# A graph layer on one core: transposes of node windows by a DRAM round trip and VectorE, and six units' rows fetched one by one from SyncE's queue

## The chip, the cores and the metric

The kernel runs on one core of a Trainium2 chip. The metric is the device time of one execution in microseconds (us). Engines are named as in the profile: PE (TensorE, matmuls), PEld (its weight loads), DVE (VectorE), ACT (ScalarE), POOL (GpSimd), SP (SyncE, which here issues DMAs; SPq is its DMA queue).

## The reference

One layer of a graph network with N = 6250 nodes, D = 256 features and E = 206250 edges that are sorted by their destination `dst`:

```python
h = jnp.maximum(_layernorm(x, axis=-1), 0.0)
polarity = jnp.clip(edge_attr[:, 0:1], 0.0, 1.0)
raw = edge_attr[:, 1:]                                  # [E, 64]
e = jax.nn.relu(raw @ W_e1.T + b_e1) @ W_e2.T + b_e2
gated = e * (polarity + 0.01)
edge_emb = gated @ W_le.T + b_le
msg = jax.nn.relu(h[src] + edge_emb)                    # [E, 256]
aggr = jax.ops.segment_sum(msg, dst, num_segments=N)
g = (h + aggr) @ W_g1.T + b_g1
mu, var = mean and variance of g over its row
hn = (g - mu) * jax.lax.rsqrt(var + LN_EPS) * ln_g + ln_b
out = x + jax.nn.relu(hn) @ W_g2.T + b_g2
```

All data are float32. W_e2 and W_le have only a scaling by edge between them, so the kernel multiplies with one product of the two (`wc_s`).

## The kernel before

**Edges.** Edges are laid in tiles of 128. A *unit* is 2 tiles, a *block* 2 units, a *group* L = 6 blocks, that is GU = 12 units; there are 806 units in 67 full groups and a rest. The main loop runs over units, `u` from LEAD = 22 to 805. For each unit stand, in the order of the engines' work:

- POOL gathers the rows `h[src]` of a unit out of DRAM (`hb_d`), with two indirect DMAs (L722), into one of 25 buffers: 17 named `hg`, 8 named `hx`. They are issued about two groups ahead, whenever a buffer is free, and a buffer is free again when the sums (L806) have read it.
- PE makes relu's argument of the first layer (L338), three pairs of units at once at the end of each group; ACT (L353) and DVE (L350) move the results out of PSUM to `e`.
- PE multiplies `e` with `wc_s` (L372: four matmuls of a unit, eight records in the profile) into a PSUM bank that ACT has filled with the bias (L402, "seed").
- DVE multiplies with the polarity and adds the gathered rows, in place (L755, two instructions a unit); ACT applies relu (L766, one instruction).

At the last unit of a group (`u % 12 == 11`) PE adds the messages up by destination (L806): 64x32 selection matrices, which DVE has built (L737), times messages. ACT (L824) and DVE (L825) move the sums into `ms`. SP then writes them to DRAM (`sum_d`), in four DMAs of 32 rows whose addresses come out of registers (`rows_out`: L905 loads the registers, L910 writes); the program makes each of the four wait for the one before. SP also clears later parts of `sum_d` (L899).

The first KEPT = 24 units are different: their products stay in tiles `msg`, because PE makes them while `h` is not yet in DRAM. Units 8 to 23 of them get their rows later, by ordinary POOL gathers set into the stream "beside" every EVERY = 36th unit, from unit 42 to 582; DVE and ACT finish them then (`whole_kept`, L778).

**Nodes.** Nodes are treated in *windows* of 128 rows. When all groups that touch a window are added up, `far_work(w)` lays out its steps over the next units. There are 47 such windows. 42 use the ordinary pools; 5 use tiles of kept units that are free by then (L173 and L214 read `msg` there), and 3 of these 5 are "filling": their last two steps are kept for the end of the program. The steps are: load `x`, and the relu of its norm (L941); load the sums (L943, SP); add both (L946, DVE, two instructions); then

- `turned`: PE transposes the [128 x 256] tile `stb` by two matmuls with an identity (L173), and ACT copies the result from PSUM to SBUF (L177, `hT`);
- `one`: the first product with `wg_s` (L188, two matmuls, four records), DVE adds the bias (L196) and takes the row statistics;
- `rooted`, `normed`: the norm (L207, L208, result `hs`);
- `two`: PE transposes `hs` (L214, two matmuls), and ACT applies scale, bias and relu on the way out of PSUM (L218, two instructions, `nT`);
- `three`: the second product (L227, four records), DVE adds `x` (L232), SP writes the output (L235).

**What sets the order.** A recording layer fixes the order of instructions on each engine as the Python code calls them; every engine then runs its list in order and waits by semaphores. Steps of windows are called after a unit's own work: `soon(n, f)` calls `f` n units later, `at(u, f)` puts it in a list of which one entry is called for each unit, and none in the units where `u % 12` is 11 or 0 (`due`). The stages above are chained by `run` with gaps of (2, 1, 1, 2, 3) units, from 12 units after the window is complete, so that a window's stages all follow one group's sums.

## Time and profile before

| | us |
|---|---|
| three runs | 3829.58, 3826.62, 3807.94 (median 3826.62) |
| the profiled execution | 3820.48 |
| its span in the profile | 3818.7 |
| PE busy | 3030.0 (79%) |
| DVE busy | 1315.3 (34%) |
| ACT busy | 1295.4 (34%) |
| POOL busy | 1563.9 (41%) |

The mean granted clock of PE was 0.789. The span is the time from the first to the last profiled instruction; the 1.8 us between it and the execution's time lie around it. A row of the timeline reads: start, duration, engine, line, operation, output<-input, shape, count, and in brackets the idle time just before it and what ended that. Engine rows of one kind that follow each other are merged, so "x4" with 5.50 us holds four instructions and what lay between them. In a row of the groups, the numbers behind the bar are the busy time of all, the mean of one in ns, and the idle time ahead of them with its releasers. "remote" and "issue" are waits for which the profile shows no engine.

### The profile page before, as it was taken

The page shows a single profiled execution, that of the slowest core. Times are in us where ns is not written, and L with a number is a line of the kernel's source. Part 1 is how long each engine was busy: PE and PEld are TensorE (multiplying, and loading weights), DVE is VectorE, ACT ScalarE, POOL GpSimd, SP SyncE. Part 2 cuts the span into 40 slices and gives each one's busy share as a digit, 9 for nine tenths or more (in the row PEclk, how much of TensorE's full clock was granted, in tenths as well). Part 3 has the DMA queues.
Part 4 walks back from the last instruction along what each step waited for, and adds up shares of the span by engine and source line. Part 5 has one row for each costly group of instructions (what it writes and reads, how often), then busy time and mean ns, then how long its engine had stood idle before and what let it go on. Part 6 is the DMA issues. An engine that isn't in the chain of part 4 may idle for free.

```text
span 3818.7 us, 51854 instructions
## 1 busy us (share of the span) xinstructions
PE 3030.0 (79%) x19998; PEld 1840.7 (48%) x19998; DVE 1315.3 (34%) x2970; ACT 1295.4 (34%) x2408; POOL 1563.9 (41%) x1674
## 2 busy tenths in 40 slices
PE   8477787788787787788787788787787888787788
PEld 5344454454455454454455455455454455455446
DVE  5343233242233232233233233233233343233234
ACT  5243233243233232333233233233242343233234
POOL 7434434424434434434433434433434434433431
PEclk9787787787787787787787787787787787787788
DMA  7322222223223222223322222322222222222321
GB/s 252 103 74 81 83 85 84 84 74 92 87 79 89 85 81 79 83 79 90 90 82 77 86 80 83 95 82 73 89 82 88 83 82 81 86 82 79 88 76 44
DMA packets 143718, 331.53 MB, mean 87 GB/s; under 512 B 36000, under 2 KB 71417, under 8 KB 142713
## 3 DMA queue, kind: packets, MB, share of 16 engines
q0 software_dynamic: 77376, 211.39, 19.2%
q1 hardware_dynamic: 64788, 113.47, 9.7%
q8 instruction: 159, 2.61, 0.3%
q10 hardware_dynamic: 1300, 3.29, 0.3%
q14 instruction: 95, 0.77, 0.1%
HBM read 306.25 MB, written 34.08 MB: 89 GB/s over the span
## 4 chain that ended last, share of the span: by engine, by line
PE 66%; another core or an unknown queue 16%; issue 14%; DVE 2%; ACT 2%; DMA 1%; POOL 0%; DVEq 0%; ACTq 0%; POOLq 0%
PE pz L372 41%; PE pz L806 13%; PE pz L338 9%; PE pz L188 1%; PE pz L227 1%; PE pz L173 1%; DVE hg L755 1%; ACT hg L766 1%; ACT pz L402 0%; PE pz L214 0%; ACT ms L824 0%; DVE sel L737 0%; DVE msg L778 0%; DMA hg<-hb_d,src_s 0%
## 5 line engine op out<-in xcount | busy, mean ns | idle before, releaser
L372 PE MATMUL pz<-wc_s,e 128*128 128x256 f32 x6448 | 1857.5, 439 | 407.0 <-issue 331.4
L372 PEld LDWEIGHTS pz<-wc_s,e 128*128 128x128 f32 x6448 | 1387.7, 220 | 861.4 <-issue 589.3
L722 POOL DMA_INDIRECT hg<-hb_d,src_s x1096 | 1038.3, 947 | 1394.3 <-PE pz L806 856.6
L722 POOL DMA_INDIRECT hx<-hb_d,src_s x500 | 473.6, 947 | 789.5 <-PE pz L806 461.3
L825 DVE TENSOR_TENSOR ms<-ms,pz 128x256 f32<-128x256 f32 x68 | 28.7, 421 | 1842.9 <-remote 715.0
L806 PE MATMUL pz<-hg,sel 64*32 64x256 f32 x4312 | 520.6, 406 | 174.7 <-issue 147.1
L824 ACT ACTIVATE ms<-pz 128x256 f32<-128x256 f32 x68 | 26.0, 383 | 1791.0 <-remote 1700.4
L755 DVE SCALAR_TENSOR_TENSOR hg<-pz,pol_s,hg 128x256 f32<-128x256 f32 x1078 | 467.4, 479 | 352.9 <-PE pz L372 90.2
L766 ACT ACTIVATE hg<-hg 128x512 f32<-128x512 f32 x538 | 337.7, 628 | 401.3 <-DVE hg L755 351.8
L402 ACT ACTIVATE pz<-bc_s 128x512 f32<-128x512 f32 x782 | 453.2, 586 | 0.0
L806 PEld LDWEIGHTS pz<-hg,sel 64*32 64x32 f32 x4312 | 164.8, 108 | 487.9 <-issue 457.8
L338 PE MATMUL pz<-raw,we_s 64*32 64x512 f32 x6448 | 377.5, 596 | 7.8 <-DVE hg L755 5.0
L350 DVE TENSOR_SCALAR e<-pz,vecs 128x512 f32<-128x512 f32 x395 | 296.3, 751 | 106.3 <-remote 24.6
L806 PE MATMUL pz<-hx,sel 64*32 64x256 f32 x1944 | 263.4, 407 | 82.5 <-issue 71.7
L353 ACT ACTIVATE e<-pz,vecs 128x512 f32<-128x512 f32 x411 | 272.6, 683 | 96.3 <-PE pz L338 40.5
L755 DVE SCALAR_TENSOR_TENSOR hx<-pz,pol_s,hx 128x256 f32<-128x256 f32 x486 | 211.8, 479 | 161.0 <-PE pz L372 49.7
L338 PEld LDWEIGHTS pz<-raw,we_s 64*32 64x32 f32 x6448 | 116.4, 107 | 226.5 <-issue 127.0
L766 ACT ACTIVATE hx<-hx 128x512 f32<-128x512 f32 x243 | 152.6, 628 | 189.9 <-DVE hx L755 165.8
L806 PEld LDWEIGHTS pz<-hx,sel 64*32 64x32 f32 x1944 | 81.1, 108 | 230.1 <-issue 217.3
L173 PE MATMUL pz<-ident,stb 128*128 128x128 f32 x84 | 25.6, 403 | 84.5 <-issue 63.9
L737 DVE SCALAR_TENSOR_TENSOR sel<-iota_w,zero_c,rel 128x256 f32<-128x256 f32 x202 | 92.6, 477 | 0.0
L173 PEld LDWEIGHTS pz<-ident,stb 128*128 128x128 f32 x84 | 13.4, 196 | 105.3 <-issue 79.5
(136 smaller groups left out, 741.8 us busy)
## 6 DMA issues: line engine op xcount, KB each, us to landing
raw<-in_raw_t_dram SPq DMA_DIRECT2D x99, 512.0 KB
hg<-hb_d,src_s POOLq DMA_INDIRECT x1096
sum_d<-zero_d SPq DMA_DIRECT2D x47, 256.0 KB
ab<-sum_d SPq DMA_DIRECT2D x42, 256.0 KB
sum_d<-ms SPq DMA_DIRECT2D x264, 32.0 KB
hx<-hb_d,src_s POOLq DMA_INDIRECT x500
hb_d<-hb SPq DMA_DIRECT2D x12, 512.0 KB
xt<-in_x_dram SPq DMA_DIRECT2D x11, 512.0 KB
```

Source lines behind the costliest of these rows:

```text
L173: z = nc.tensor.transpose(pt[:, 0, c * P:c * P + n], a[:n, c * P:(c + 1) * P], ident[:n, :n])
L188: z = nc.tensor.matmul(ph[:n, 0, :], aT[:, c, :n], wg1_s[:, c, :], start=c == 0 and not bias_by_pe, stop=c == 1)
L338: z[c] = nc.tensor.matmul(bank[s, c].tile[j * W:(j + 1) * W].rearrange("p a b -> p (a b)"), we1_s[s * F:(s + 1) * F, c * P + j * W:c * P + ...
L350: a = nc.vector.tensor_scalar(e1[b][:, c, :], pe, be1_s[:, c:c + 1], 0.0, op0=ALU.add, op1=ALU.max)
L353: a = nc.scalar.activation(e1[b][:, c, :], pe, AF.Relu, bias=be1_s[:, c:c + 1])
L372: z = nc.tensor.matmul(bank.tile[:, i, :], e1[b][:, c, k:k + P], wc_s[:, c, :], start=not seeded and i == c == 0, stop=c == 1, skip_group_ ...
L402: a = nc.scalar.activation(bank.tile, bc_s, AF.Copy)
L722: g = nc.gpsimd.indirect_dma_start(out=hg[u][:, i, :], out_offset=None, in_=hb_d, in_offset=bass.IndirectOffsetOnAxis(ap=src_s[:, 2 * u + ...
L737: nc.vector.scalar_tensor_tensor(sel[g][:, k * S:k * S + n, :], iota_w.rearrange("p (o w) -> p o w", o=1).to_broadcast([P, n, W]), zero_c, ...
L755: product = nc.vector.scalar_tensor_tensor(hg[u][:, i, :], bank.tile[:, i, :], pol_s[:, 2 * u + i:2 * u + i + 1], hg[u][:, i, :], op0=ALU. ...
L766: done[u] = product, nc.scalar.activation(hg[u], hg[u], AF.Relu)
L806: z = nc.tensor.matmul(acc[g][h][j * W:(j + 1) * W, :], sel[g][h * F:(h + 1) * F, k * S + j, :], m[h * F:(h + 1) * F, j % 2, :], start=k = ...
```

## The change

There are two parts, and some code around them.

**Transposes.** For 44 windows both transposes, and for the 3 filling ones the first, leave PE. SP writes the tile to one of eight DRAM tiles `turn_d` (L1008, 128x256). Two units later it issues four DMAs (L1014), each of which reads the 32x32 blocks of it for 32 partitions of a tile `pm` (runs of 32 numbers, that is 128 bytes, 256 runs to a DMA): block (i, j) comes to the place of block (j, i), still with its own rows. Three units later DVE turns each 32x32 block in itself (L1019, one STREAM_TRANSPOSE of 128x256), into `hT` or `nT`. For `nT` ACT applies scale, bias and relu in SBUF (L228, two instructions). The pool `pm` has two buffers. The line of a window is then longer than one group: the first write stands at the last unit of a group, the first product six units later, the second write three units after it, and the second product four units after the next group's sums.

**Rows.** Units 8 to 13 of the kept ones are no longer gathered by POOL. From unit 63 on a buffer is taken for one of them at a time (`place_of_rows`), and after every second unit SP loads six row numbers into registers (L767) and issues six DMAs of one row each (1 KB, L772, each with register instructions ahead of it, "ISA" below). The lists of numbers come from a new input `src_r` (L748). A unit has 256 rows, so it takes 86 units; the last is done near unit 608. The ten others stay with POOL, now every 60th unit from 54 to 594.

Around these: some early tiles lie in a pool of their own that is closed sooner, and an early group counts as complete by the number of its finished units. POOL's gathers in the main part fall from 1596 to 1584, PE's list falls from 5123 rows to 5032, and DVE's rises from 2240 to 2331. Lines of the kernel before keep their work under new numbers: L188 -> L191, L227 -> L236, L372 -> L381, L722 -> L734, L755 -> L811, L766 -> L822, L806 -> L862, L824 -> L880, L825 -> L881, L910 -> L967, L943 -> L1000.

The core of the diff:

```diff
-EVERY = 6 * L
+EVERY = 5 * GU
+ROWS = 6
+BY_ROW = 6
...
+    turn_d = [dram.tile([P, D], F32, name=f"turn_d{i}") for i in range(8)]
...
+        def relu_of(nT):
+            for c in range(2):
+                a = nc.scalar.activation(nT[:, c, :], nT[:, c, :], AF.Relu, bias=lnb_s[:, c:c + 1],
+                                         scale=lng_s[:, c:c + 1])
+            return nT, a
...
-            for r in range(RAW, KEPT):
-                i = KEPT + EVERY * (r - RAW) + EVERY // 2
+            for n, r in enumerate(range(RAW + BY_ROW, KEPT)):
+                i = KEPT + EVERY * n + EVERY // 2
...
+            def place_of_rows(u):
+
+                if u > LEAD + 40 and single and single[0][0] not in hg and free:
+                    hg[single[0][0]] = free.popleft()[0]
...
+            def some_rows(u):
...
+                n = min(ROWS, P - at_row)
+                _, found = nc.values_load_multi_w_load_instructions(
+                    listed[r, i][0:1, at_row:at_row + n], engines=[mybir.EngineType.SP], min_val=0, max_val=N - 1,
+                    skip_runtime_bounds_check_because="a row of a node")
+                for k in range(n):
+                    p = at_row + k
+                    nc.sync.dma_start(out=hg[r][p:p + 1, i, :], in_=hb_d[bass.ds(found[k], 1), :])
+                at_row += n
...
+                def out_rows(a):
+                    box["d"] = turn_d[len(turned_rows) % len(turn_d)]
+                    turned_rows.append(w)
+                    nc.sync.dma_start(out=box["d"], in_=a)
+
+                def in_blocks():
+                    box["pm"] = pm.tile([P, 2 * S, W], F32, name="pm")
+                    rows = box["d"].rearrange("(b i) (c a j) -> a i c b j", i=W, a=S, j=W)
+                    for q in range(S):
+                        nc.sync.dma_start(out=box["pm"][q * W:(q + 1) * W].rearrange("i (c b) j -> i c b j", c=2),
+                                          in_=rows[q])
+
+                def blocks_turned(name, pool):
+                    t = pool.tile([P, 2, P], F32, name=name)
+                    nc.vector.transpose(t.rearrange("p c n -> p (c n)"), box["pm"].rearrange("p q j -> p (q j)"))
+                    return t
...
-                stages = [turned, one, rooted, normed, two, three]
+                line = [(first_out, 2, True), (in_blocks, 3, True), (turned, 1, False), (one, 1, False),
+                        (rooted, 1, False), (normed, 1, False), (second_out, 2, True), (in_blocks, 3, True),
+                        (second_turned, 2, False), (three, 0, False)]
+                if filling:
+                    line = line[:6]
...
-                    if i < len(stages) - (3 if filling else 1):
-                        at(now + (2, 1, 1, 2, 3)[i], lambda: run(i + 1))
+                    if i < len(line) - 1:
+                        if line[i + 1][2]:
+                            soon(line[i][1], lambda: run(i + 1))
+                        else:
+                            at(now + line[i][1], lambda: run(i + 1))
...
+                place_of_rows(u)
                 gathers()
+                if u > LEAD + 40 and u % 2 == 0:
+                    some_rows(u)
```

How it moves instructions is seen in each engine's order at three places. The first is PE, just behind a group's sums. Before, a window's two transposes (L173, L214) and its two products (L188, L227) all stand between the products L372 of six units:

```order
L806 MATMUL pz_148<-hg_863,sel_140 32x256
L372 MATMUL pz_144<-wc_s,e_102 128x256 x4
L372 MATMUL pz_146<-wc_s,e_102 128x256 x4
L173 MATMUL pz_145<-ident,stb 128x128 x2
L372 MATMUL pz_142<-wc_s,e_103 128x256 x4
L372 MATMUL pz_147<-wc_s,e_103 128x256 x4
L188 MATMUL pz_148<-wg_s,hT 128x256 x2
L372 MATMUL pz_149<-wc_s,e_104 128x256 x4
L372 MATMUL pz_143<-wc_s,e_104 128x256 x4
L372 MATMUL pz_144<-wc_s,e_105 128x256 x4
L372 MATMUL pz_146<-wc_s,e_105 128x256 x4
L214 MATMUL pz_145<-ident,hs 128x128 x2
```

Now the same place reads:

```order
L862 MATMUL pz_157<-hg_881,sel_148 32x256
L381 MATMUL pz_152<-wc_s,e_110 128x256 x4
L381 MATMUL pz_154<-wc_s,e_110 128x256 x4
L381 MATMUL pz_153<-wc_s,e_111 128x256 x4
L381 MATMUL pz_156<-wc_s,e_111 128x256 x4
L236 MATMUL pz_155<-wg_s,nT 128x256 x2
L381 MATMUL pz_150<-wc_s,e_112 128x256 x4
L381 MATMUL pz_151<-wc_s,e_112 128x256 x4
L191 MATMUL pz_157<-wg_s,hT 128x256 x2
```

The transposes are gone. The second product (L236), of the window before, stands behind four units, and the first (L191), of the next window, behind six.

The second place is SP's queue at the end of a group (L905, now L962, loads the registers for the rows of the sums). Before:

```order
L235 DMA out_dram<-ot 128x256
L320 DMA raw<-in_raw_t_dram 128x1024 x2
L905 TENSOR_LOAD base_i
L910 ISA
L910 DMA sum_d<-ms 32x256
L910 ISA
L910 DMA sum_d<-ms 32x256
```

Now (`turn_d_64` holds the window's sums, `hg_891` is the buffer of a unit that is fetched by rows; the last two of six rows stand at the top):

```order
L772 ISA
L772 DMA hg_891<-hb_d 1x256
L962 TENSOR_LOAD base_i
L967 ISA
L967 DMA sum_d<-ms 32x256
L967 ISA
L967 DMA sum_d<-ms 32x256
L967 ISA
L967 DMA sum_d<-ms 32x256
L967 ISA
L967 DMA sum_d<-ms 32x256
L1014 DMA pm<-turn_d_64 32x8x32 x4
```

Six rows with their loads stand ahead of the writes of the sums, the four reads for the window's first transpose behind all four of them, and then, not shown, the next six rows.

The third place is DVE and ACT behind the sums' eviction (L881 on DVE, L880 on ACT). Before, neither has an instruction of a transpose here. Now DVE turns `nT` behind the second unit's L811, and `hT` three units later:

```order
L881 TENSOR_TENSOR ms<-ms,pz_157 128x256
L793 SCALAR_TENSOR_TENSOR sel_148<-iota_w,zero_c,rel 128x256 x2
L811 SCALAR_TENSOR_TENSOR hg_893<-pz_152,pol_s,hg_893 128x256 x2
L793 SCALAR_TENSOR_TENSOR sel_148<-iota_w,zero_c,rel 128x256
L811 SCALAR_TENSOR_TENSOR hg_894<-pz_154,pol_s,hg_894 128x256 x2
L1019 STREAM_TRANSPOSE nT<-pm 128x256
L811 SCALAR_TENSOR_TENSOR hx_116<-pz_153,pol_s,hx_116 128x256 x2
L811 SCALAR_TENSOR_TENSOR hx_117<-pz_156,pol_s,hx_117 128x256 x2
L241 TENSOR_TENSOR ot<-pz_155,xt_8947 128x256
L811 SCALAR_TENSOR_TENSOR hg_878<-pz_150,pol_s,hg_878 128x256 x2
L1019 STREAM_TRANSPOSE hT<-pm 128x256
```

ACT's relus of `nT` (L228) stand behind the second unit's relu (L822), and ahead of the next seed (L411).

More of the change, by code (lines that the diff above doesn't have):

```diff
@@ L933, in far_work @@
                 box = {}
[L934 removed]
+                turn, first, root, scaled, second, relu_of, third, load_x, offset = finish_nodes(nd, ps, w, P)
                 def h_of_x():
@@ L978, in far_work @@
                 if filling:
-                    fillers.append(stages[-2:])
-                at(now + 12, lambda: run(0))
+                    fillers.append((two, three))
+                soon(12, lambda: run(0))
             def at_last(box):
@@ L1167, in gnn_kernel @@
                     fn()
-            assert not moves
+            assert not moves and not single and not ready
             while steps:
@@ L1305, in nodes @@
             nc.sync.dma_start(out=ac[:n], in_=acc_d[bass.ds(w * P, n), :])
-            turn, one, root, scaled, two, three, load_x, offset = v["finish_nodes"](sk, Fresh(), w, n)
+            turn, one, root, scaled, two, _, three, load_x, offset = v["finish_nodes"](sk, Fresh(), w, n)
             xt = load_x()
```

65 lines of the change are left out of this document (50 added, 15 removed).

## The prediction

> **What bounds the kernel now.** I read four views in this order: the page's chain of work that ended last, the busy time by windows over a few neighbouring groups, the waits, and the timeline of one group's end. The chain first:
>
> ```profile
> PE 66%; another core or an unknown queue 16%; issue 14%; DVE 2%; ACT 2%; DMA 1%; POOL 0%; DVEq 0%; ACTq 0%; POOLq 0%
> ```
>
> TensorE carries two thirds, but 30% is "an unknown queue" and "issue", time that the chain can't put down to an engine. Where it lies is seen when the windows are laid from one eviction of the sums (L825) to the next (columns: length, then busy us and count of PE, PEld, DVE, ACT, POOL; PE clock, DMA share, GB/s):
>
> ```profile
> 1514.50:1541.50 27.00, 26.00 (x186) 19.36 (x193) 17.20 (x39) 16.45 (x31) 0.94 (x1) 0.95 0.17 49
> 1541.50:1573.70 32.20, 19.15 (x121) 8.47 (x106) 1.05 (x3) 2.28 (x5) 21.73 (x23) 0.66 0.36 107
> 1573.70:1598.60 24.90, 24.90 (x176) 18.50 (x182) 17.81 (x39) 16.54 (x29) 2.84 (x3) 0.90 0.17 45
> 912.90:940.20 27.30, 17.92 (x117) 7.16 (x102) 0.96 (x3) 1.49 (x4) 17.78 (x19) 0.63 0.34 104
> 3769.20:3800.00 30.80, 30.13 (x229) 23.47 (x227) 17.55 (x46) 16.71 (x32) 0.00 (x0) 1.00 0.08 18
> ```
>
> A group has two stretches. In the fast one PE is busy to the last microsecond, at a clock of 0.90 to 0.95, with all node work in it. In the slow one POOL issues 19 or 23 gathers while PE crawls through its 120 matmuls at 0.63 to 0.66, and DVE and ACT have three to five instructions. A last group with no gather at all takes 30.8 us for everything, against 27.0 + 32.2 = 59.2 for the first here. So the gathers beside the sums set the slow stretch and PE sets the fast one; work that PE loses pays only in the fast one. The slow stretch ends in the one great wait, in a longer and a shorter form:
>
> ```profile
> ACT ms L824 <- remote: 1700.4, 60, 32.6
> 1572.20 0.38 ACT L824 ACTIVATE ms<-pz 128x256 f32<-128x256 f32 x1 [29.64 <-remote]
> 939.50 0.38 ACT L824 ACTIVATE ms<-pz 128x256 f32<-128x256 f32 x1 [25.64 <-remote]
> ```
>
> **What the transposes give back.** A window's PE work stands in the fast stretch (PE timeline of one window):
>
> ```profile
> 1513.54 0.69 PE L173 MATMUL pz<-ident,stb 128*128 128x128 f32 x2 [2.71 <-issue]
> 1514.03 5.39 PE L372 MATMUL pz<-wc_s,e 128*128 128x256 f32 x16
> 1520.42 1.13 PE L188 MATMUL pz<-wg_s,hT 128*128 128x256 f32 x4 [1.00 <-ACT hT L177]
> 1521.39 7.07 PE L372 MATMUL pz<-wc_s,e 128*128 128x256 f32 x32
> 1528.30 0.38 PE L214 MATMUL pz<-ident,hs 128*128 128x128 f32 x2
> 1528.52 1.68 PE L372 MATMUL pz<-wc_s,e 128*128 128x256 f32 x7
> ```
>
> ```profile
> L173 PE MATMUL pz<-ident,stb 128*128 128x128 f32 x84 | 25.6, 403 | 84.5 <-issue 63.9 <-ACT ms L824 20.6
> L214 PE MATMUL pz<-ident,hs 128*128 128x128 f32 (+1 forms) x88 | 16.8, 273 | 0.1
> L188 PE MATMUL pz<-wg_s,hT 128*128 128x256 f32 (+1 forms) x176 | 48.5, 399 | 17.5 <-ACT hT L177 12.9 <-ACT hg L766 2.9 <-ACT hx L766 0.9
> ```
>
> The starts tell what a pair of transposes costs the stream: L214 at 1528.30, the next product at 1528.52, so 0.22 us; L173 at 1513.54, the next at 1514.03, so 0.49 (the clock is still low there). The change takes 47 pairs of L173 and 44 of L214 (of 47 windows; three keep the second on PE): 47 x 0.49 + 44 x 0.22 would be 33 us. But L173 stands where PE comes out of the slow stretch and waits for other things anyhow (84.5 us of idle time are booked ahead of it), so I count it at half: **-21 us**. Second, L188 today waits for ACT's copy of hT, 17.5 us in its row: that copy goes, **-17 us**. ACT's copies and DVE's 91 new turns are off the limit: in a fast stretch of 27 us DVE is busy 17.2 and ACT 16.5.
>
> **What the round trip costs.** It needs no more of PE, but two things now come later, and PE, which runs in order, stops for each with the whole stream of products behind it. This is a group's end (ACT, DVE, and SP's DMA queue together; L825 is the zero, 1573.67; two L755 make a unit):
>
> ```profile
> 1573.67 0.42 DVE L825 TENSOR_TENSOR ms<-ms,pz 128x256 f32<-128x256 f32 x1 [31.05 <-ACT pz L402]
> 1574.12 2.84 SPq L910 DMA_DIRECT2D sum_d<-ms  x2
> 1576.46 0.88 DVE L755 SCALAR_TENSOR_TENSOR hx<-pz,pol_s,hx 128x256 f32<-128x256 f32 x2 [1.58 <-remote]
> 1577.65 0.87 DVE L755 SCALAR_TENSOR_TENSOR hg<-pz,pol_s,hg 128x256 f32<-128x256 f32 x2
> 1578.11 1.78 SPq L910 DMA_DIRECT2D sum_d<-ms  x2
> 1578.44 0.86 DVE L755 SCALAR_TENSOR_TENSOR hx<-pz,pol_s,hx 128x256 f32<-128x256 f32 x2
> 1578.55 0.63 ACT L766 ACTIVATE hg<-hg 128x512 f32<-128x512 f32 x1
> 1579.78 0.88 DVE L755 SCALAR_TENSOR_TENSOR hg<-pz,pol_s,hg 128x256 f32<-128x256 f32 x2 [0.47 <-ACT pz L402]
> 1581.06 0.36 SPq L943 DMA_DIRECT2D ab<-sum_d  x1
> 1583.23 0.88 DVE L755 SCALAR_TENSOR_TENSOR hx<-pz,pol_s,hx 128x256 f32<-128x256 f32 x2 [0.85 <-ACT hx L766]
> L946 DVE TENSOR_TENSOR stb<-stb,ab 128x256 f32<-128x256 f32 x84 | 34.9, 416 | 0.0
> L218 ACT ACTIVATE nT<-pz,vecs 128x128 f32<-128x128 f32 (+1 forms) x88 | 34.7, 444 | 1.4 <-PE pz L214 1.4
> ```
>
> *nT, for the second product.* In the new order DVE's turn of nT stands behind the second unit's L755 after L825, ACT's two relus behind that unit's L766, and PE wants nT after the fourth unit. The second unit's L755 ends at 1577.65 + 0.87 = zero + 4.9. The turn isn't in the trace; its nearest row is L946 with the same tile size, 0.42, and I take 0.45: 5.3. ACT's L766 ends at 1579.18, zero + 5.5; then two relus of 0.44 by L218: nT is whole at zero + 6.4. PE ends its fourth unit no later than DVE starts on it, 1579.78 = zero + 6.1: a wait of 0.3. In another group PE is further ahead of DVE:
>
> ```profile
> 2139.54 4.96 PE L372 MATMUL pz<-wc_s,e 128*128 128x256 f32 x16
> 2144.07 0.87 DVE L755 SCALAR_TENSOR_TENSOR hx<-pz,pol_s,hx 128x256 f32<-128x256 f32 x2
> 2145.93 1.13 PE L188 MATMUL pz<-wg_s,hT 128*128 128x256 f32 x4 [1.43 <-ACT hT L177]
> PE pz L188 <- ACT hT L177: 12.9, 14, 1.4
> ```
>
> There PE ends the fourth unit at 2139.54 + 4.96 = 2144.50, and DVE the second only at 2144.94; with 0.45 and 2 x 0.44 nT is whole at 2146.27: a wait of 1.8. It is such a group where today L188 waits for its hT, and by the last row (total, count, longest) there are 14 of them. So (14 x 1.8 + 28 x 0.3) / 42 = 0.8 us a window.
>
> *hT, for the first product.* In SP's new order the four reads into pm stand behind the four L910 writes of sum_d, each of which waits until the one before has landed (two in 2.84, so 1.42 each). The last is issued by 1578.11 + 1.78 = zero + 6.2. Four reads at 0.36 (L943's issue) make 7.7. From issue to landing I take one whole step of L910's chain, 1.42, an issue and a landing of as many bytes: 9.1; the turn 0.45: 9.5, and about 0.3 for two handovers. PE wants hT two units after nT, zero + 9.6 (the L755 at 1583.23), or 9.9 if nT has held it by 0.3: no wait. But each read comes in 256 runs of 128 bytes where L910 has 32 rows; if that takes twice the step, 1.3. Between the two I take 0.6 in the 28 windows where PE isn't held long for nT: 28 x 0.6 / 42 = 0.4.
>
> So a window costs 0.8 + 0.4 = 1.2 us; 0.3 where both just fit; 0.8 + 1.4 = 2.2 where short runs are slow everywhere. Over the 44 windows that do both: **+53 us**, bounds 13 and 97. Below nothing it can't go: the old wait is already taken off. The write of h to DRAM (L1008), the write of hs and the second pm read stand in or ahead of the slow stretch, units before their use: no cost.
>
> The Trainium skill speaks against this part. "DMA: Bandwidth & Descriptors", Rules for kernel authors, wants a transpose left to the hardware's DMA transpose and not to a plain DMA with a rearranged access pattern, which it puts 19 times slower; "VectorE: DVE Perf Modes", The three transpose paths, has the same factor, for a large innermost destination stride. By its 1.3 us for the hardware path a turn would take an estimated 25 us. Here 32 neighbouring numbers stay together at both ends, so I hold its condition as not met; no row of this trace has such a transfer.
>
> **The six units fetched by SyncE.** Two POOL gathers for each of six units go, 12 in all:
>
> ```profile
> 1562.46 0.94 POOL L722 DMA_INDIRECT hg<-hb_d,src_s  x1 [0.30 <-issue]
> 1563.71 0.95 POOL L722 DMA_INDIRECT hg<-hb_d,src_s  x1 [0.30 <-issue]
> 1541.87 0.33 SPq L320 DMA_DIRECT2D raw<-in_raw_t_dram  x1
> 1574.12 0.36 SPq L910 DMA_DIRECT2D sum_d<-ms  x1
> ```
>
> One gather is 1.25 us from start to start: 12 x 1.25 = 15 us if all stood in slow stretches, nothing if in fast ones, where the windows above hold POOL's few gathers without a loss to PE. An ordinary period still has its 24. I take **-3 us**. In place of them SP issues 1536 rows, six in every second unit, so 36 a group over some 44 groups. From the last two rows: SP's queue issues nothing from 1541.87 to 1574.12, 32 us of each group. A row is at least an issue of 0.36 and at most one step of L910's chain, 1.42 (if each waited for the landing before it). Its order shows no wait of a row for the row before, so I take 0.5: 36 x 0.5 = 18 us beside SP's other work of about 12 (L910 5.5, the four-part reads and short issues some 6) in 57: hidden. At 1.42 it is 51 + 12 = 63 us, 6 too many in each of 44 groups, +260 us. The rows hold one of 25 buffers until unit 608; gathers run a group ahead of their use, so nothing is late.
>
> **Sum:** 3820.5 (the profiled execution; span 3818.7) - 21 - 17 + 53 - 3 = **3832 us**. The median of the runs is 3826.6, 0.2% above that execution, and I make no correction for it. The 1% that a measurement tells from no change is 38 us: faster is below 3788, slower above 3865.
>
> **Rivals.**
> *A, the data are in time.* Short runs land as fast as long ones, and PE, which no longer has L173 ahead of its units, is no more ahead of DVE than at 1579: 0.3 a window, 13 us, and all 12 gathers count: 3820.5 - 38 + 13 - 15 = 3780. For it: in 28 of 42 windows the sums miss by only 0.3. Against: L188 waits today for one short ACT copy alone (12.9 of its 17.5), so there is no slack at this place even now. 0.24.
> *B, both products wait, on the other side.* The reads of short runs come in series behind sum_d, 2.2 us a window, 44 x 2.2 = 97, and DVE's turn and ACT's relus each come behind one more unit's work (0.88 and 0.63, 44 x 1.5 = 66): 3820.5 - 41 + 163 = 3943. It is slower by 1% from (44.5 + 41) / 44 = 1.9 us a window on (44.5 from 3820.5 to 3865). For it: DVE and ACT take instructions in order and hold L755 and L402 there. Against: it needs every window late. 0.22.
> *C, the stretches change their mix.* All 60 L824 waits long: 60 x 29.64 = 1778, +78 us; all short: 60 x 25.64 = 1538, -162. One buffer fewer and 12 fewer gathers may shift which form a group takes; nothing in the trace says which way. 0.09: half of it faster at about 3750, half slower at about 3880.
> *D, SP becomes the bound,* a row at 1.42: 3832 + 260 = 4090. For it: L910's register-addressed writes do take that. Against: they wait for each other by order, the rows don't. 0.04.
> *E, a read costs by its runs:* 256 runs for 32 rows is 8 steps of 1.42, 11.4 us in place of 1.42; hT comes 10 us late in each window, 44 x 10 = 440: 4270. 0.02. The Trainium skill's 19-fold rule above goes the same way.
> *F, the change doesn't do what it says:* the gathers that go were hidden and the transposes too, and nothing new waits, 3820; it lies inside the forecast's own range.
>
> **How the numbers follow.** The forecast has 0.39: 3832, own range 3790 to 3880 (the wait between 0.3 and 2.2 a window). A 0.24, B 0.22, C 0.09, D and E 0.06. Range for 8 in 10: from 3765 (A with the full 33 us of transposes, 3768) to 3920 (B with 43 of its 66 us). Faster: 0.17 of A's 0.24, 0.05 of C and 0.03 of the forecast's lower edge, 0.25. Slower: B 0.22, D and E 0.06, C 0.04 = 0.32, less B's lower edge 0.02 = 0.30. Same: 0.45.
>
> **What would show it.** L191's and L236's idle time "from DVE hT" and "ACT nT": my sum wants 53 us there, A under 20, B over 120. The turn of 128x256 on DVE should be near 0.45 us. The windows' fast stretch should shorten by at most 0.8 where nothing waits, and the slow one should stay at 27 or 32. SP's row issues should be near 0.5 us apart, with L910 no later than 0.5 us behind L825. I am wrong if the fast stretch moves by more than 1.5 us a group, if L824's waits change by more than 40 us, or if SP is busy up to L825.

## The result

| | us |
|---|---|
| the change, four runs | 3947.88 to 3968.07, median 3960.54 |
| the kernel before, beside them | 3807.94 to 3833.0, median 3828.1 |
| ratio | 1.0353, 95% interval 1.0306 to 1.0400 |
| span of the profiled execution | 3966.4 (before 3818.7) |

The change costs 3.5%, 132 us by the medians and 148 between the two profiled executions. I had forecast no change that can be told, 3832, with 3920 as the upper end.

The windows of the change again run from one eviction of the sums (now L881) to the next, each group cut where its sums (L862) begin:

```profile
837.70:865.20 27.50, 26.00 (x199) 19.29 (x203) 20.38 (x47) 17.58 (x32) 3.07 (x3) 0.95 0.23 64
865.20:889.30 24.10, 18.88 (x110) 7.67 (x95) 0.79 (x2) 1.14 (x3) 16.10 (x17) 0.65 0.48 143
889.30:926.80 37.50, 28.22 (x195) 20.85 (x201) 18.11 (x41) 17.37 (x32) 6.64 (x7) 0.86 0.22 55
926.80:959.00 32.20, 21.58 (x123) 8.50 (x106) 0.88 (x3) 2.11 (x5) 21.81 (x23) 0.68 0.36 105
```

The first and the last row could stand in the kernel before. The two between could not: a slow stretch of 24.1 us with 17 gathers, and a fast one of 37.5 with 7, in which PE is busy for 28.2 only. The groups of the change say on what PE stands; the last row is the kernel before, where the second product (L227) waited for nothing:

```profile
L236 PE MATMUL pz<-wg_s,nT 128*128 128x256 f32 (+1 forms) x176 | 65.1, 505 | 177.4 <-ACT nT L228 176.4 <-issue 0.7
L191 PE MATMUL pz<-wg_s,hT 128*128 128x256 f32 (+1 forms) x176 | 49.4, 405 | 19.2 <-DVE hT L1019 18.5 <-DVE msg L834 0.4
L1019 DVE STREAM_TRANSPOSE hT<-pm 128x256 f32<-128x256 f32 x42 | 18.4, 439 | 23.8 <-DMA pm<-turn_d 23.8
L1019 DVE STREAM_TRANSPOSE nT<-pm 128x256 f32<-128x256 f32 x42 | 18.2, 434 | 2.1 <-DMA pm<-turn_d 2.1
L228 ACT ACTIVATE nT<-nT,vecs 128x128 f32<-128x128 f32 x84 | 36.3, 478 | 1.9 <-DVE nT L1019 1.9
L227 PE MATMUL pz<-wg_s,nT 128*128 128x256 f32 (+1 forms) x176 | 46.2, 385 | 0.0
```

The second product waits 177 us for nT, though the blocks of nT are there (2.1 us of DVE's turns waiting for them) and the turn is short. Most of it comes in 19 of the 47 windows, of which one stands in the third stretch above. These are its rows, by engine: PE and DVE first, then ACT, POOL and SP's queue.

```profile
887.61 5.88 PE L381 MATMUL pz<-wc_s,e 128*128 128x256 f32 x24
902.77 2.08 PE L236 MATMUL pz<-wg_s,nT 128*128 128x256 f32 x4 [9.28 <-ACT nT L228]
```

```profile
889.26 0.42 DVE L881 TENSOR_TENSOR ms<-ms,pz 128x256 f32<-128x256 f32 x1 [23.25 <-ACT ms L880]
898.92 0.88 DVE L811 SCALAR_TENSOR_TENSOR hg<-pz,pol_s,hg 128x256 f32<-128x256 f32 x2 [8.84 <-remote]
900.41 0.87 DVE L811 SCALAR_TENSOR_TENSOR hg<-pz,pol_s,hg 128x256 f32<-128x256 f32 x2 [0.22 <-remote]
901.20 0.43 DVE L1019 STREAM_TRANSPOSE nT<-pm 128x256 f32<-128x256 f32 x1
```

```profile
901.86 0.86 ACT L228 ACTIVATE nT<-nT,vecs 128x128 f32<-128x128 f32 x2
```

```profile
889.39 0.95 POOL L734 DMA_INDIRECT hx<-hb_d,src_s  x1 [0.30 <-issue]
...
896.92 0.95 POOL L734 DMA_INDIRECT hg<-hb_d,src_s  x1 [0.31 <-issue]
```

```profile
873.09 8.29 SPq L772 DMA_DIRECT2D hg<-hb_d  x6
889.71 6.21 SPq L967 DMA_DIRECT2D sum_d<-ms  x4
895.92 2.94 SPq L1014 DMA_DIRECT2D pm<-turn_d  x4
900.29 2.37 SPq L772 DMA_DIRECT2D hg<-hb_d  x6
```

PE's rows place the fourth unit's matmuls before 893.5. Yet DVE's first L811 of the group stands idle for 8.84 us. It waits there for PE's product and for a gather that was issued two groups earlier; so I take it that PE's notice (the semaphore by which DVE learns that the product is there) is late, though the profile names no engine. It comes at 898.9, behind the end of POOL's seventh gather (897.87). The turn of nT stands two units behind that L811 in DVE's order, ACT's relus behind the turn, and L236 behind the relus. PE, which in the kernel before ran on with the next units in such a place, now stops until the whole chain is through.

SP's four reads (L1014) end at 898.86, so they could hold up the notice as well. All places of this form decide between the two: in 20 of 23 the second unit's L811 starts only 10 to 12 us behind L881, after POOL's run of gathers has ended (at 7.4 to 9.7), and five of these 20 have no reads there.

In the 62 whole periods of each profile I counted POOL's issues between the first L862 and the next L881. The periods fall into three forms (slow stretch + the fast one behind it, means in us). Left out are the first period, those beside the two places where kept units are added up, and in the change two near the end with 10 and 8 gathers and fast stretches of 46 and 47 us:

| gathers in the slow stretch | before | the change |
|---|---|---|
| 21 to 24 | 37 times, 32.1 + 26.6 = 58.7 | 32 times, 32.4 + 27.3 = 59.7 |
| 19 or 20 | 22 times, 27.2 + 26.8 = 54.0 | 2 times, 27.0 + 28.4 = 55.4 |
| 15 to 18 | none | 23 times, 24.2 + 35.3 = 59.5 |

The short form of the kernel before, 54 us, has become one with still fewer gathers in the slow stretch and 7 in the fast one, and that form is not short at all. 23 x 5.5 = 127 us and 32 x 1.0 = 32 make 159, a rough account of the 148 measured.

The counts 17 and 19 are what fits in before L881. POOL's first pause, in which it waits for a free buffer, comes earlier still: after 12.5 gathers on the mean of the slow stretches that have SP's rows beside them (SP issues rows from 337 to 3009 us), against 17.4 in the same profile where no rows run and 17.5 in the kernel before. A buffer is free again when the sums have read it, and the sums are behind. These are L862's matmuls (L806's in the last row) in the first 15 us of a slow stretch, with rows, without, and in the kernel before (columns: length, PE busy and count, PEld, clock, DMA share, GB/s):

```profile
864.94:879.94 15.00, 10.34 (x78) 2.90 (x71) 0.71 0.59 177
3379.71:3394.71 15.00, 10.95 (x94) 3.10 (x86) 0.74 0.44 132
912.86:927.86 15.00, 10.71 (x95) 3.29 (x88) 0.74 0.38 119
```

On the mean PE has done 82 of its 96 by then in the 44 stretches with rows, and 95 in the 16 others and in the kernel before. All 23 stretches with 15 to 18 gathers lie among the 44, and none among the 16; so do 156 of the 177 us at L236. The one great wait at the end of the slow stretches is shorter than before (1700.4, 60, 32.6):

```profile
ACT ms L880 <- remote: 1414.6, 52, 32.7
```

### The profile page after: what moved, and what is told of

Its sections match the earlier page's. It is cut to its first block, busy times and chain, and to the rows that moved or that the text cites. A ratio compares the mean times of both kernels' runs of the same rounds, so it can differ in the third digit from the quotient of the medians.

```text
span 3966.4 us, 57296 instructions
## 1 busy us (share of the span) xinstructions
PE 2990.8 (75%) x19816; PEld 1837.4 (46%) x19816; DVE 1345.8 (34%) x3061; ACT 1286.7 (32%) x2361; POOL 1556.8 (39%) x1662
## 4 chain that ended last, share of the span: by engine, by line
PE 28%; another core or an unknown queue 14%; issue 10%; SPq 2%; DMA 2%; DVE 1%; ACT 1%; DVEq 0%; ACTq 0%
PE pz L381 17%; PE pz L347 5%; PE pz L862 4%; PE pz L236 1%; DMA sum_d<-ms 1%; PE pz L191 1%; DMA pm<-turn_d 1%; SPq L1014 1%; SPq L772 0%; DVE hg L811 0%; ACT nT L228 0%; DVE sel L793 0%; SPq L967 0%; ACT hg L822 0%
## 5 line engine op out<-in xcount | busy, mean ns | idle before, releaser
L381 PE MATMUL pz<-wc_s,e 128*128 128x256 f32 x6448 | 1730.6, 429 | 365.6 <-issue 158.1
L381 PEld LDWEIGHTS pz<-wc_s,e 128*128 128x128 f32 x6448 | 1385.0, 218 | 729.6 <-issue 276.2
L734 POOL DMA_INDIRECT hg<-hb_d,src_s x1072 | 1018.5, 950 | 1744.2 <-PE pz L862 1228.9
L862 PE MATMUL pz<-hg,sel 64*32 64x256 f32 x4240 | 592.5, 429 | 276.9 <-issue 249.6
L734 POOL DMA_INDIRECT hx<-hb_d,src_s x512 | 486.1, 949 | 594.8 <-PE pz L862 307.2
L811 DVE SCALAR_TENSOR_TENSOR hg<-pz,pol_s,hg 128x256 f32<-128x256 f32 x1060 | 459.2, 477 | 496.1 <-remote 192.9
L881 DVE TENSOR_TENSOR ms<-ms,pz 128x256 f32<-128x256 f32 x68 | 28.7, 421 | 1727.5 <-ACT pz L411 645.4
L880 ACT ACTIVATE ms<-pz 128x256 f32<-128x256 f32 x68 | 26.1, 384 | 1670.7 <-remote 1414.6
L822 ACT ACTIVATE hg<-hg 128x512 f32<-128x512 f32 x529 | 332.0, 628 | 640.4 <-DVE hg L811 533.3
L862 PEld LDWEIGHTS pz<-hg,sel 64*32 64x32 f32 x4240 | 175.9, 111 | 661.4 <-issue 630.3
L411 ACT ACTIVATE pz<-bc_s 128x512 f32<-128x512 f32 x782 | 451.4, 583 | 0.0
L862 PE MATMUL pz<-hx,sel 64*32 64x256 f32 x2016 | 278.6, 422 | 117.0 <-issue 103.4
L811 DVE SCALAR_TENSOR_TENSOR hx<-pz,pol_s,hx 128x256 f32<-128x256 f32 x504 | 219.0, 478 | 190.9 <-PE pz L381 70.8
L822 ACT ACTIVATE hx<-hx 128x512 f32<-128x512 f32 x252 | 157.9, 627 | 225.7 <-DVE hx L811 218.5
L862 PEld LDWEIGHTS pz<-hx,sel 64*32 64x32 f32 x2016 | 85.3, 110 | 265.1 <-issue 252.4
L236 PE MATMUL pz<-wg_s,nT 128*128 128x256 f32 (+1 forms) x176 | 65.1, 505 | 177.4 <-ACT nT L228 176.4
L236 PEld LDWEIGHTS pz<-wg_s,nT 128*128 128x128 f32 (+1 forms) x176 | 39.3, 242 | 195.8 <-ACT nT L228 189.1
```

Of the source, the lines that this page charges most:

```text
L236: z = nc.tensor.matmul(po[:n, 0, :], nT[:, c, :n], wg2_s[:, c, :], start=c == 0, stop=c == 1)
L381: z = nc.tensor.matmul(bank.tile[:, i, :], e1[b][:, c, k:k + P], wc_s[:, c, :], start=not seeded and i == c == 0, stop=c == 1, skip_group_ ...
L411: a = nc.scalar.activation(bank.tile, bc_s, AF.Copy)
L734: g = nc.gpsimd.indirect_dma_start(out=hg[u][:, i, :], out_offset=None, in_=hb_d, in_offset=bass.IndirectOffsetOnAxis(ap=src_s[:, 2 * u + ...
L811: product = nc.vector.scalar_tensor_tensor(hg[u][:, i, :], bank.tile[:, i, :], pol_s[:, 2 * u + i:2 * u + i + 1], hg[u][:, i, :], op0=ALU. ...
L822: done[u] = product, nc.scalar.activation(hg[u], hg[u], AF.Relu)
```

## The experiments

The experiments didn't all meet the same condition: at e1 to e4, e9 to e13 and e15 to e17 every kernel is much faster, the one before takes 2115 us with PE's clock near 1.0 and no slow stretch at all (seen in the profile of e9, which has one buffer less). So each run is told with its ratio to the kernel before, timed beside it, and its 95% interval.

Theory 1 after the result was the chain above: PE stops at the products since nT's turn is queued behind L811, whose notices are late while POOL gathers. Theory 2 was that the rows lose it.

**e1, the round trip alone** (again as e11 and e15), and **e2, the rows alone** (again as e12 and e16).

```diff
 e1: -EVERY = 5 * GU          e2: far_work's stages as in the kernel before
     +EVERY = 6 * L
     -BY_ROW = 6
     +BY_ROW = 0
```

> The round trip alone; units 8 to 13 go back to POOL's gathers, 16 of them beside every 36th unit as before. Theory 1 (the time is lost where PE stops at the second product L236: nT's turn stands on DVE behind the first two units' L811, which wait for PE's notices while POOL still gathers): nearly all of the loss stays, 3930 to 3965 us, L236's idle time 140 us or more. Theory 2 (the rows by SyncE lose it, by the buffer they hold and by SP's time, and the transposes alone come out near my sum): 3815 to 3850 us, L236's idle time under 60.

> The rows by SyncE alone; all transposes are PE's again, in the places of the kernel before. Theory 1: within 1% of the kernel before, 3805 to 3845 us. Theory 2: 3930 us or more.

Where the kernel before takes 2115 us, e1 is 1.0543 (1.0519 to 1.0568) and e2 1.0230 (1.0206 to 1.0253) times as long. Both parts lose there, each by a wait of its own. In e1 it is the first product that waits, for hT, and hT for the reads behind the sums' writes (groups, then SP, DVE and PE in one place):

```profile
L191 PE MATMUL pz<-wg_s,hT 128*128 128x256 f32 (+1 forms) x176 | 62.6, 488 | 101.1 <-DVE hT L1019 101.1
L236 PE MATMUL pz<-wg_s,nT 128*128 128x256 f32 (+1 forms) x176 | 45.3, 380 | 0.0
```

```profile
1034.36 2.87 SPq L967 DMA_DIRECT2D sum_d<-ms  x2
1037.34 2.54 SPq L1014 DMA_DIRECT2D pm<-turn_d  x4
1041.87 0.45 DVE L1019 STREAM_TRANSPOSE hT<-pm 128x256 f32<-128x256 f32 x1 [3.37 <-DMA pm<-turn_d]
1042.37 1.13 PE L191 MATMUL pz<-wg_s,hT 128*128 128x256 f32 x4 [3.12 <-DVE hT L1019]
```

A read's issue takes 2.54 / 4 = 0.64 us where I took 0.36, and the last one needs 2.0 us more to be seen by DVE where I took 1.42: 1.7 us late by these two alone. The Trainium skill ("DMA: Bandwidth & Descriptors", Anatomy of one DMA) has about 2.0 us fixed for a DMA, stated for POOL's queue; this row on SP's is near it, with 2.0 us from the end of the last issue and 2.6 from its start. The Trainium skill's 19-fold rule for transposing reads (same page, Rules for kernel authors) isn't seen: 4.5 us from the first issue to the turn, not 25.

In e2 the rows put SP's other loads off (waits: total, times, longest; in e9, a kernel without rows in this condition, neither wait is there):

```profile
ACT stb L998 <- DMA xt<-in_x_dram: 103.2, 31, 8.5
DVE stb L1003 <- DMA ab<-sum_d: 97.5, 31, 5.1
```

**e3, nT turned early,** with three buffers of `pm` in place of two.

```diff
-(second_out, 2, True), (in_blocks, 3, True), (second_turned, 2, False), (three, 0, False)]
+(second_out, 2, True), (in_blocks, 1, True), (second_turned, 4, True), (three, 0, False)]
```

> The whole change, but DVE turns nT one unit after its blocks are read, which puts the turn and ACT's two relus right behind the sums' L881 and L880 and ahead of the first two units' L811 and L822; pm has three buffers in place of two. PE's order is that of the change. Theory 1: L236's idle time falls from 177 to under 20 us; hT's turn still stands behind five units' L811, so part of the wait comes back at L191 (19 us now, then 40 to 90): 3820 to 3900 us. Theory 2: no gain beyond 20 us, 3940 us or more, since the wait at L236 only shows time that is lost elsewhere.

It ran in the 2115 us condition and is the slowest of all, 1.1627 (1.1599 to 1.1655). There nT was never late (L236 in e1: 0.0). DVE's turn of nT now waits 49 us, nearly all for its reads, with the next units' L811 behind it, and L191's wait is 243 us. How much of the loss is the rows', which e1 lacks, isn't known, as the whole change wasn't timed there. The run doesn't test theory 1, since nothing waits there that it could mend.

**e4, the change without the rows' DMAs.**

```diff
-                for k in range(n):
-                    nc.sync.dma_start(out=hg[r][p:p + 1, i, :], in_=hb_d[bass.ds(found[k], 1), :])
+                if at_row == 0:
+                    nc.sync.dma_start(out=hg[r][0:P, i, :], in_=hb_d[0:P, :])
```

> The whole change without the fetch of single rows: each list loads its registers, but one DMA of 128 rows stands in place of 128 single ones, so the six units get other rows than the reference's; the buffer is held as long as before. Theory 1: as the change, 3940 to 3965 us. Theory 2 by SP's time or the row transfers: 3815 to 3850 us; by the held buffer: as the change.

It leaves the fetch of the single rows out: 128 other rows come in one DMA. 1.0554 (1.0532 to 1.0575), the same as e1. In the 2115 us condition a held buffer and loaded registers cost nothing beside the round trip, which leaves the 36 DMAs a group for what the rows lose there.

**e5 to e8** met the condition of the result, on the chip of e1 to e4. e5 is the change again, e6 the kernel before with a profile, e7 has both products later, e8 the reads for hT one unit earlier:

```diff
 e7: -(turned, 1, False)          e8: -(first_out, 2, True), (in_blocks, 3, True)
     +(turned, 3, False)              +(first_out, 1, True), (in_blocks, 4, True)
     -(second_turned, 2, False)
     +(second_turned, 5, False)
```

> The change itself, on the chip of this call. Where the kernel before takes 2115 us as in the first four runs, the losses of the two parts there (118 us for the transposes, 48 for the rows) add up if they are separate: 2260 to 2290 us; if both are waits in the same place they overlap: 2225 to 2250. Where the kernel before takes 3828 us: 3945 to 3970 again.

> The kernel before, for its profile on the chip of this call. Theory 1 says that POOL's gathers don't slow PE on the chip of the first four runs: no stretch with a clock under 0.9 and no wait of ACT L824 above 5 us, and L188's wait under 25 us; then the 2.0 us between the two chips at each gather are all that makes the 1700 us. Theory 2: the same two stretches as in the first profile, only shorter.

> The whole change with both products later: L191 eight units after the sums in place of six, L236 seven or more in place of four. Theory 1 (PE stops because the data of the two products aren't there, L191 by the reads behind the sums' writes, L236 by the turn behind L811): L191's and L236's idle times fall under 30 us together, and the time falls by 60 to 110 us against the change on the same chip. Theory 2 (PE loses the time to transfers and queues wherever the products stand): within 25 us of the change.

> The whole change with the four reads for hT one unit earlier, so that they stand behind two of the four L967 in place of all four. Theory 1, where L191 is the one that waits (the chip of the first four runs): two steps of the chain less, 2.8 us, L191's idle time under 40 us and 50 to 90 us faster than the change. Where L236 waits (the chip of the first profile): within 25 us of the change. Theory 2: within 25 us of the change on either.

e5 is 1.0383 (1.0332 to 1.0435), 3962 against 3819; e6 1.0027 (0.9986 to 1.0068), with its slow stretches and 1644 us of L824's waits as in the first profile, so it doesn't tell of the other condition. e7 is 1.0182 (1.0128 to 1.0235): 77 us of the 143 come back, as theory 1 expected, and no wait is left at either product. But 66 us stay, and e7's groups show that PE now stops more in the stream itself, above all for ACT's seeds (L411), which stand behind the relus of the late units in ACT's order. The last row is e5's:

```profile
L381 PE MATMUL pz<-wc_s,e 128*128 128x256 f32 x6448 | 1739.6, 431 | 447.7 <-ACT pz L411 188.4 <-issue 184.4 <-ACT ms L880 57.7
L236 PE MATMUL pz<-wg_s,nT 128*128 128x256 f32 (+1 forms) x176 | 46.3, 386 | 2.9 <-issue 2.9
L191 PE MATMUL pz<-wg_s,hT 128*128 128x256 f32 (+1 forms) x176 | 46.2, 385 | 0.0
L381 PE MATMUL pz<-wc_s,e 128*128 128x256 f32 x6448 | 1721.5, 428 | 307.7 <-issue 179.4 <-ACT pz L411 84.2 <-ACT ms L880 35.2
```

The products' waits are 225 us shorter than in e5, and the stream's 140 longer; the time falls by 77.

```profile
1021.60:1045.60 24.00, 16.46 (x114) 6.47 (x99) 0.93 (x2) 2.19 (x5) 15.67 (x17) 0.64 0.42 123
1045.60:1079.70 34.10, 27.74 (x192) 20.62 (x198) 17.87 (x41) 16.31 (x30) 7.03 (x8) 0.95 0.25 70
```

The same form again, 17 gathers and then a fast stretch of 34 us. So the wait at L236 is only where the late notices show; theory 1 explains where PE stops, not why the gathers have moved. e8 is 1.0315 (1.0263 to 1.0367), 23 us less than e5: it takes L191's wait from 30 to 6 us. L236's is 155 in place of 199, but no more than the 23 us are seen in the time.

**e9, the kernel before with 24 buffers, and e14, the change with 26.** Theory 3: POOL pauses sooner because the rows hold a buffer.

```diff
 e9: -HG = 17 + RAW          e14: -HG = 17 + RAW
     +HG = 16 + RAW               +HG = 18 + RAW
```

> The kernel before with 24 buffers for gathered rows in place of 25; nothing else. Theory 3 (the buffer that the rows hold makes POOL pause two gathers sooner in the slow stretch, 17 in place of 19, and these gathers then hold up PE's notices in the fast stretch): where the kernel before takes 3820 us, 40 to 110 us slower, with a fast stretch above 28 us on the mean in place of 26.6. Rival (the buffer is no matter, gathers run a group ahead): within 20 us. Where it takes 2115 us, gathers don't hold PE, and both expect less than 25 us.

> The whole change with 26 buffers for gathered rows in place of 25; nothing else. Theory 3 (the buffer held by the rows is what moves gathers into the fast stretch): where the kernel before takes 3820 us, at least 60 us faster than the change's 3962, 3820 to 3900 us, with a fast stretch of 28.5 us or less on the mean in place of 30.9. Rival (the buffer is no matter): 3940 to 3980, the stretches as in the change. Where the kernel before takes 2115 us the number of buffers makes no difference (e9), so this gives the whole change there: the sum of the parts' losses, 113 and 48 us, is 2275 us; less if they overlap.

e9 fell in the 2115 us condition: 0.9998 (0.9988 to 1.0007), as both theories had it there. e14 met the condition of the result, on another chip: 1.0293 (1.0251 to 1.0336), 0.9 points or 34 us better than e5, where theory 3 wanted 60. By the two intervals it is 0.2 to 1.6 points. Of its slow stretches with rows 17 still have 15 to 18 gathers, and POOL's first pause comes as early as in the change (after 11.9), with 81 of PE's 96 matmuls done after 15 us. Theory 3 falls as the main cause; the buffer gives some quarter of it. Part of that lies at the end: from unit 756 on the change takes 18 us more than the kernel before, with the two fast stretches of 46 and 47 us, and e14, which has none there, 1 us more.

**e10, e13 and e17, later products with the rows and 26 buffers, and without the rows** (e17 is e13 once more).

> The whole change with both products later, as e7, and 26 buffers in place of 25, so that 25 are left beside the one that the rows hold. Theory 3: where the kernel before takes 3820 us, what is left over of the loss (66 us in e7) goes for the most part, 3780 to 3830 us. Rival (SP's rows and the reads themselves cost it): within 20 us of e7's 3885. Where the kernel before takes 2115: within 25 us of what later products alone give there.

> The round trip alone, with both products later, 25 buffers and no rows. Where the kernel before takes 3820 us: with the waits at both products gone (theory 1, e7) and no buffer held (theory 3), nothing of the loss is left and the transposes' place on PE is free: 3775 to 3825 us. Rival (the 66 us left in e7 come from the reads and from what moves behind them, not from the rows or their buffer): 3860 to 3890. Where it takes 2115: without the rows SP has its reads out in time, so L191's and L236's idle times fall under 20 us, 2105 to 2150 us; if the stages that stand later collide with the next group's, above 2250.

> The round trip alone with both products later, in the same condition. If the waits at the products are all that the round trip costs: 0.99 to 1.00 times the kernel before, since PE's transposes and the old wait for hT are gone. If the round trip also lengthens the fast stretch otherwise: 1.01 or more.

All three fell in the 2115 us condition. e13 is 1.0080 (1.0056 to 1.0104) and e17 1.0069 (1.0050 to 1.0088): without rows, two units more for hT take L191's wait from 101 to 9 us and nearly all of the round trip's loss with it. e10 is 1.1445 (1.1421 to 1.1470). By e9 the buffers make no difference there, so rows and round trip together cost far more than each alone (1.023 and 1.008). e10's own groups say the same: 37.3 us each from unit 72 to 612, while rows run, and 31.6 in the ten groups from unit 636 to 756, behind the last row (e13: 31.1 and 30.9). DVE's turns for hT wait 297 us for their reads in e10, 153 in e13. That SP's queue has no room for both in a group of 31 us would fit; it wasn't tested by itself. The whole change itself wasn't timed in that condition.

**e11, e12, e15, e16** were meant to split the loss in the condition of the result, and met the other: 1.0517, 1.0232, 1.0530 and 1.0233, as e1 and e2. The rows alone were never timed in the condition of the result.

> The round trip alone, 25 buffers, no rows. Where the kernel before takes 3820 us: theory 1 with theory 3 has L236's wait come mostly from the long rest of gathers, so without the rows it is a third or less of the change's 204 us, and the time lies near my first sum, 3810 to 3860 us. Theory 1 alone (the place of nT's turn loses it, rows or not): 3890 to 3930. Where it takes 2115: 2232 again.

> The rows alone, transposes on PE. Where the kernel before takes 3820 us: theory 3 has it 40 to 110 us slower, as with one buffer less (e9), and within 25 us of that run; theory 1 alone: within 30 us of the kernel before. Where it takes 2115: 2162 again.

> The round trip alone, in the condition of the recorded result if it holds on. The change is 143 us slower there, 26 buffers make it some 30 less. If the round trip carries the rest: 1.025 to 1.035 times the kernel before, L236's idle time 120 us or more. If the rows carry it: 1.010 or less.

> The rows alone in the same condition. If the round trip carries the loss: 0.995 to 1.010 times the kernel before. If the rows carry what later products leave (66 us): 1.012 to 1.025.

**e18, the round trip alone with the reads half ahead:** e8 without the rows.

> The round trip alone, with the reads for hT one unit earlier, so that they stand behind two of the four L967 (as e8, without the rows). Where the kernel before takes 3820 us: e8 was 1.0315 times the kernel before; if the round trip carries the loss, this is 1.022 to 1.032, if the rows carry it, 1.010 or less. Where it takes 2115 us: the round trip alone was 1.053 there, with 98 us of waits for hT at L191; if these waits come from the reads' place behind the sums' writes, they fall below 50 us and the ratio to 1.015 to 1.035; if the reads' own length makes them, it stays above 1.045.

It met the condition of the result: 1.0099 (1.0062 to 1.0135), 3895 against 3855. Its groups, and the windows of two neighbouring periods:

```profile
L236 PE MATMUL pz<-wg_s,nT 128*128 128x256 f32 (+1 forms) x176 | 52.7, 425 | 32.9 <-ACT nT L228 17.4 <-issue 15.2
L191 PE MATMUL pz<-wg_s,hT 128*128 128x256 f32 (+1 forms) x176 | 45.9, 383 | 7.4 <-DVE hT L1019 7.4
```

```profile
892.24:918.62 26.38, 26.38 (x185) 19.83 (x191) 18.57 (x43) 17.04 (x31) 2.88 (x3) 0.91 0.22 53
918.62:945.41 26.79, 17.62 (x115) 6.72 (x100) 0.95 (x3) 1.59 (x4) 17.24 (x19) 0.67 0.34 102
945.41:975.28 29.87, 27.85 (x186) 20.65 (x193) 17.35 (x38) 17.32 (x32) 5.51 (x6) 0.90 0.24 71
975.28:1008.04 32.76, 18.77 (x120) 8.33 (x104) 0.96 (x2) 1.24 (x4) 21.90 (x24) 0.66 0.38 109
```

19 and 24 gathers: the two forms of the kernel before are back. No period of e18 has 15 to 18, and none in the two profiles of the kernel before. In each of the five profiles with rows in this condition, 15 to 23 of the 44 or 45 slow stretches beside rows have, and at most two of the others. POOL's first pause in e18 comes after 16.2 gathers.

Against e8 the rows are worth 1.0315 - 1.0099 = 2.2 points, 83 us with an interval of some 24 either way. e8 and e18 ran on two chips, on which the kernel before takes 3819 and 3855 us; the ratio takes it that this difference carries over to the changed kernels. If it doesn't, the plain times give 45 us. From unit 72 to 612 a group takes 59.7 us in e8 and 58.4 in e18, and behind the rows, from 636 to 756, 57.4 and 58.2. So by the two profiles, 61 us apart in all, e8's loss against e18 lies where rows run, 55 us, and behind unit 756, 20 us. What is left to the round trip, 38 us here and 23 more by e8 against e5, is 61 by the ratios, and by the plain times it would be larger by as much as the rows are smaller.

## Why the prediction was wrong

- **The rows were costed at nothing, since they fit into SP's time; this is the step that failed,** with -3 in the sum where some +83 was measured (e8 against e18; 45 by the plain times), and 48 where the kernel before takes 2115 us (e2). The fit itself held: a row in the fast stretch is 2.37 / 6 = 0.40 us, under my 0.5, though 8.29 / 6 = 1.38 in the slow one. What I never priced is what six DMAs at a time do to PE in a stretch where SP had been still. While they run, PE has done 82 of its 96 matmuls of the sums after 15 us, in place of 95; the buffers come free later, POOL pauses after 12.5 gathers in place of 17.4, and in half of these groups six or seven gathers are left for the fast stretch.
- **The round trip** stood at -21 - 17 + 53 = +15, and 61 was measured (e18, and e5 against e8). So it was too cheap as well, though the turn, the order and the waits were the ones that I had named.
- **The stretches** were read rightly: gathers set the slow one, PE the fast one. The sentence that fails is that the fast windows "hold POOL's few gathers without a loss to PE". It holds for the five that the short form before leaves at the start of the stretch: the second unit's L755 starts there 2.9 to 5.7 us behind L825. With six or seven it starts 10 to 12 us behind L881 in 20 of 23 places, when POOL is through.
- **The mix of the stretches** was my rival C, at 0.09, and it is what happened, in a way that I had not seen. I priced it by L824's wait alone, as if the fast stretch kept its length. Over the 67 periods the slow stretches became shorter by 113 us, and the fast ones longer by 263. Two of my signs of being wrong came with it: the fast stretch moved by 4 us a group, and the wait of L880 (before: L824) by 286 us, or by 120 with what is booked to other releasers.
- **The wait for nT** had the right place and order (second unit's L811, turn, relus, L236) and the wrong size, 0.8 us a window or 35 us, against 177. Without the rows it is 33 (e18): the sum was made for groups as they stood before, and the rows changed the groups.
- **The wait for hT** was 18 us in the sum and 19 in the profile (30 in e5); the turn 0.45 us and 0.44. The 1.42 us of a step were misread: the row of 2.84 us holds one whole step and a second issue, and by their starts the steps are 2.49, 1.50 and 1.47. The landing, for which I took 1.42, is 2.0 in e1.
- **The old wait and the transposes** can't be seen apart from the rest; e18 has 40 us of waits at the products and is 38 us slower than the kernel before, so some of the 38 us that I let come back did not, or went elsewhere.
- **Rival B** gave 3943 and was nearly the time, for a reason that isn't its own, which is luck: it needs every window late by 2.2 us or more, and here 19 of 47 wait for 3 us and more, up to 19, and the others hardly.
- **Rival D**, SP as the bound, is not what happened here; in the 2115 us condition e10 against e13 speaks for it.

What stays open is how SP's row DMAs slow PE's sums, and with what they collide; no run takes that apart. Open too is the exact share of rows and round trip in the 143 us, as above.

## What to carry to other kernels

An idle queue isn't free room for DMAs: ask what runs beside it at that time, and whether that is limited by what the DMAs also use. Before a step is costed by the places of other work in an old trace, ask whether the change moves these places. When a matmul's operand gets a new producer, look at what stands ahead of the producer on its engine; a late notice there, that nobody minded, becomes a stop of PE.

## What the hardware showed

The same kernel has two conditions, 3820 and 2115 us, and one chip showed both within a quarter of an hour (e1 to e4, then e5 to e8). What sets the condition isn't known. In the slower, PE crawls while POOL gathers: 120 matmuls in a stretch of 32 us. In the faster it doesn't, with 24 gathers in a window in which PE is busy throughout (e1, PE clock 1.00):

```profile
997.20:1026.10 28.90, 28.90 (x276) 22.09 (x266) 18.34 (x41) 18.87 (x35) 21.89 (x24) 1.00 0.49 143
```

The Trainium skill ("SBUF — State Buffer", SBUF: two separate sides) says that a DMA can't slow a compute operation and that PE never waits for anyone there. The second condition agrees, with PE busy for all of the 28.90 us; in the first PE stands still beside gathers, and more so beside SP's rows (78 of the sums' matmuls in 15 us, in place of 94), and where it waits these runs don't tell.
